# A two-layer graph kernel: row sums taken from counts, two accumulators for adj, broadcasts by transfers, and smaller edits

## The chip, the cores and the metric

The kernel runs on one core of one Trainium2 chip. The metric is the device time of one execution in microseconds. A core has five instruction streams that matter here: TensorE (PE, matrix products and transpositions), VectorE (DVE), ScalarE (ACT), GpSimd (POOL), and SyncE (SP), whose stream issues nearly all DMA transfers of this kernel. Each stream runs its instructions in program order, and waits on semaphores where an operand comes from another stream.

## What is computed

The input is `x` (3327 nodes, 256 features) and `adj` (3327 x 3327, about 0.5% of it non-zero, and the diagonal). There are two layers, each with a layer norm and a relu in front and a residual sum behind. Cut to what matters:

```python
# layer 0: h = relu(layernorm(x)); R = rows of (adj + I) scaled to sum 1
Xf = Xa = h
for n in range(2):
    logits = (Xa @ W1.T @ W2.T) @ (Xa @ W3.T).T      # 3327 x 3327
    probs = softmax(logits)
    A = probs, of each row only the largest that sum to 0.9, scaled to sum 1
    Xf = R @ Xf
    Xa = A @ Xa
    Z = Z + Xf @ U1[n].T + Xa @ U2[n].T
x = x + layernorm(h + Z)
# layer 1: h = relu(layernorm(x)), 4 heads of 64 features
hp = h @ W
e = leaky_relu(s[:, :, None] + d[:, None, :], 0.2)   # s, d: per node and head
attn = softmax(where(adj > 0, e, -inf))
x = x + elu(attn @ hp)
```

## The kernel before

The nodes are padded to 3328 and cut into 26 row tiles of 128. `adj` comes transposed, so that a tile of it can be the stationary operand of a product.

The order of the work is made by a planner at build time. Each piece of work is given to `put` with an engine, a length, a rank, the pieces that it needs, and the buffers that it takes and gives back. A list scheduler walks through modelled time, and on each engine starts the piece of smallest rank whose needs are met and whose buffers are free. The pieces are then written out in that order, so the order of each engine is fixed in the program; on the chip only the waits decide. A change of one length or need may therefore move many pieces.

**Layer 0** has two steps. At the start, `prepare` makes each row tile: layer norm, relu, projection to keys and queries (128 columns, of which one half of the partitions is keys). Half of the partitions carries one group of key tiles and the other half the others, so that two products with a contraction of 64 run side by side on the two halves of the array. `keys_summed` and `moments` (lines 722 to 753) sum the keys and their products over all row tiles: a transposition (line 730), an ACT copy (line 734), a product with 65 columns (line 739), and DVE additions (line 751). From these `stats` makes, for each row, a normal model of its logits.

For each row tile and each step, `search` (line 1343) then finds the threshold on the exponentials above which a row holds 0.9 of its sum:

- `logits` (line 842): three pairs of 512 keys, each pair on both halves of the array, and the last 255 keys on one half alone; `exps` (line 853) makes the exponentials with ACT.
- `guess` sets a first threshold from the model. An evaluation is a `count` (line 890): two ACT passes over 3327 columns with the accumulated output kept, one with Relu (how much lies below the threshold, and by how much) and one with Sign (how many lie below). `step` (lines 894 to 932) then moves the threshold: a chain of small POOL operations on one column each. Step 0 has two evaluations, step 1 three. The third of step 1 is `sum_below` on DVE (line 936), with its `step` on DVE.
- In the window around the threshold DVE selects and sorts the candidates (lines 947 and 952) and drops what lies below the cut (line 1002).

`attention` transposes the row tile's exponentials (line 1015), copies them out with ACT into `et` (line 1020), and multiplies them with the features (line 1027). Between rows, PE has `Full`: 26 matmuls per row tile of the product with adj (line 1053) into the accumulator `accf`; four adj tiles come by each transfer into `at` (line 1047); ACT copies the accumulator to `f` (line 1060), and DVE adds. The planner gives `accf` back when the copy is done. `finish2` (lines 1282 to 1302) ends a row tile of step 1: layer norm, relu, projection with the weights of layer 1, and `stage`, which makes exponentials of the score of each node and head (`qd`, `low`).

**Layer 1** is `attend_neighbours` (line 1427). It has four blocks of 832 destination columns, and in each block 26 source tiles j. For each j, SP loads the adj tiles (line 1500), ACT makes a mask of them (lines 1510 and 1511), DVE makes the exponents of four heads (line 1522), and PE multiplies them (line 1538) and sums them (line 1552). The exponents need the scores of the destination columns on all partitions: for each row tile of the block, `broadcast` transposes a score column repeated 128 times (PE, line 1460) and takes its exponential into the buffer `both` (ACT, line 1464). The large buffers of layer 1 are those of layer 0: `both` is `c`, and it is opened when all adj products are done.

The layer-1 weights are loaded by `layer1_weights` (lines 700 to 720): four transfers on SP and four products on DVE (line 713), which take two of the three `et` buffers; the planner puts them near 120 us.

## Time and profile before

| | us |
|---|---|
| median of three runs | 2310.74 (2310.22 to 2312.15) |
| the profiled execution | 2309.92 |
| its span | 2307.9 |
| PE idle in the span | 84.9 |
| PE idle, 0 to 58 | 15.5 |
| PE idle, 950 to 1100 | 3.3 |
| PE idle, 1100 to 1400 | 11.1 |
| PE idle, 1400 to 1780 | 14.2 |
| PE idle, 2000 to 2308 | 17.7 |

The profile is of one execution. The span is the time between its first and its last instruction; about 2 us of the execution lie outside it. The idle time in a stretch is its length less the busy time of PE in the table of windows. The times of PE's matmuls overlap, so a group's mean is longer than the pace at which its matmuls follow each other, and a busy PE need not be at its peak. In the groups, "x208" is the number of instructions, then come the busy time in us and the mean in ns, and then the idle time of the engine just before these instructions with what ended most of it. In a list of waits, the three numbers are the sum in us, how many waits, and the longest.

### The profile page before, as it was taken

To read this page: it belongs to the slowest core of one execution; us is meant where nothing else is said; L and a number is where in the kernel's file an instruction comes from. 1 tells how busy PE (TensorE), PEld (TensorE's weight loads), DVE (VectorE), ACT (ScalarE), POOL (GpSimd) and SP (SyncE) were. 2 spreads that over 40 slices of the span, in tenths; PEclk is the share of its full clock that TensorE was granted. 3 is DMA by queue.
4 is the path that set the end of the run, shared out by engine and by line. 5 is a ranking of instruction groups with operands and counts; after the bars stand their busy time and mean duration, and the time that the engine had idled before them with its cause. 6 is when DMAs were issued, how large, how long until landed. Compare 5 with 4: busy or idle time off the path is not lost. (4 is left out here: it accounts for less than half of the span.)

```text
span 2307.9 us, 36154 instructions
## 1 busy us (share of the span) xinstructions
PE 2223.0 (96%) x11956; PEld 1551.9 (67%) x11956; DVE 1699.8 (74%) x4299; ACT 1559.9 (68%) x2901; POOL 1017.6 (44%) x2263
## 2 busy tenths in 40 slices
PE   7989999999999999999999999999998999999997
PEld 5467777777877778777777778777877434333332
DVE  5564666656645664389889889889888797989895
ACT  5767788678777862488676787777773556565553
POOL 6345455445554541357766765677774000000000
PEclk9999999999999999999999999999999999999998
DMA  3021212212212222522212222122223343434341
GB/s 97 1 68 52 68 54 60 64 53 61 73 47 72 68 87 73 176 85 65 65 51 68 68 76 67 53 62 68 71 67 99 90 114 109 116 99 127 100 130 42
DMA packets 189654, 176.97 MB, mean 77 GB/s; under 512 B 14866, under 2 KB 145808, under 8 KB 189328
## 3 DMA queue, kind: packets, MB, share of 16 engines
q1 hardware_dynamic: 187472, 173.30, 25.8%
q8 instruction: 96, 1.57, 0.3%
q10 hardware_dynamic: 1984, 1.26, 0.2%
q14 instruction: 102, 0.84, 0.1%
HBM read 157.66 MB, written 15.89 MB: 75 GB/s over the span
## 5 line engine op out<-in xcount | busy, mean ns | idle before, releaser
L890 ACT ACTIVATE junk<-e,sc 128x3327 fp8e5<-128x3327 f32 x208 | 638.9, 3072 | 25.4 <-POOL sc L931 23.4
L1027 PE MATMUL acca<-rhs,et 128*128 128x256 f32 x2704 | 623.6, 381 | 2.3 <-ACT et L1020 2.2
L1027 PEld LDWEIGHTS acca<-rhs,et 128*128 128x128 f32 x2704 | 500.6, 191 | 66.9 <-ACT et L1020 4.8
L1053 PE MATMUL accf<-c,at 128*128 128x256 f32 x1352 | 322.8, 388 | 20.4 <-ACT f L1060 20.3
L947 DVE SCALAR_TENSOR_TENSOR y<-e,sc 128x1664 f32<-128x1664 f32 x104 | 204.6, 1967 | 187.0 <-POOL sc L928 169.3
L1053 PE MATMUL accf<-main,at 128*128 128x257 f32 x1352 | 317.0, 383 | 4.8 <-DMA at<-in_adjt_dram 4.5
L1020 ACT COPY et<-px 128x512 f32<-128x512 f32 (+1 forms) x364 | 194.4, 554 | 186.4 <-PE acca L1027 125.3
L1053 PEld LDWEIGHTS accf<-c,at 128*128 128x128 f32 x1352 | 251.6, 192 | 78.4 <-ACT f L1060 28.8
L1522 DVE SCALAR_TENSOR_TENSOR e<-c,low,et 128x832 f32<-128x832 f32 x288 | 289.1, 1075 | 16.8 <-ACT e L1592 9.5
L1053 PEld LDWEIGHTS accf<-main,at 128*128 128x128 f32 x1352 | 250.9, 191 | 46.4 <-issue 8.0
L952 DVE MAX8 cands<-y 128x8 f32<-128x208 f32 x832 | 241.1, 361 | 3.6
L1002 DVE SCALAR_TENSOR_TENSOR e<-e,thr 128x832 f32<-128x832 f32 x208 | 214.0, 1083 | 2.6 <-ACT kq L1178 0.5
L1538 PE MATMUL pl<-e,main 128*64 128x416 f32 x1152 | 212.6, 516 | 0.1
L1015 PE MATMUL px<-ident,e 128*128 128x128 f32 x1352 | 196.4, 277 | 16.8 <-ACT et L1020 7.9
L853 ACT ACTIVATE e<-pl 128x1024 f32<-128x1024 f32 x208 | 179.3, 865 | 45.6 <-PE pl L842 44.7
L1015 PEld LDWEIGHTS px<-ident,e 128*128 128x128 f32 x1352 | 163.4, 143 | 57.5 <-issue 13.6
L1511 ACT ACTIVATE et<-at 128x512 bf16<-128x512 f32 (+1 forms) x208 | 114.5, 550 | 118.3 <-DVE e L1522 76.9
L842 PE MATMUL pl<-kt,qq 64*128 64x512 f32 (+1 forms) x728 | 184.1, 588 | 0.0
L905 POOL TENSOR_SCALAR sc<-sc 128x1 f32<-128x1 f32 x104 | 40.2, 386 | 309.3 <-ACT junk L890 249.3
L1538 PEld LDWEIGHTS pl<-e,main 128*64 128x64 f32 x1152 | 79.6, 137 | 123.1 <-issue 104.0
L936 DVE SCALAR_TENSOR_TENSOR y<-e,sc 128x3327 bf16<-128x3327 f32 x26 | 95.5, 3672 | 47.9 <-POOL sc L931 47.9
L1522 DVE SCALAR_TENSOR_TENSOR rhs<-c,low,et 128x832 f32<-128x832 f32 x128 | 129.2, 1073 | 0.0
(485 smaller groups left out, 3076.8 us busy)
## 6 DMA issues: line engine op xcount, KB each, us to landing
at<-in_adjt_dram SPq DMA_DIRECT2D x416, 256.0 KB, 2.8
at<-in_adjt_dram SPq DMA_DIRECT2D x104, 192.0 KB, 3.0
at<-in_adjt_dram SPq DMA_DIRECT2D x52, 128.0 KB, 2.1
ys<-ystage SPq DMA_DIRECT2D x26, 256.0 KB, 2.4
rhs<-in_x_dram SPq DMA_DIRECT2D x26, 128.0 KB, 3.3
ystage<-in_x_dram SPq DMA_DIRECT2D x26, 128.0 KB, 2.1
base<-ys SPq DMA_DIRECT2D x26, 128.0 KB, 2.2
x1s<-ystage SPq DMA_DIRECT2D x26, 128.0 KB, 1.7
```

The lines of the kernel that those rows point to most:

```text
L842: T.matmul(pl[:, r, :m], qq[half, self.i, :], kt[half, 512 * k : 512 * k + m], start=True, stop=True,)
L853: S.activation(self.e[:, 1024 * k : 1024 * k + pl.shape[1]], pl, AF.Exp, accum_out=(self.p0, self.p1, self.p2, self.p3)[k],)
L890: S.activation(junk[:, :N], self.e[:, :N], fn, bias=t, scale=-1.0, accum_out=dst, saturate=False)
L947: V.scalar_tensor_tensor(self.y[:, : hi - lo], self.e[:, lo:hi], self.up, self.e[:, lo:hi], ALU.is_lt, ALU.mult, accum_out=(self.h0, self. ...
L952: V.max(self.cands[:, o // PIECE, :], self.y[:, o - lo : min(o + PIECE, hi) - lo])
L1002: V.scalar_tensor_tensor(piece, piece, self.thr[:, o : o + 1], piece, ALU.is_gt, ALU.mult)
L1015: T.transpose(pt[:, k, :], self.e[:, j * P : (j + 1) * P], ident)
L1020: S.copy(self.et[g][:, :m, :], self.pt.pop(g)[:, :m, :])
L1027: T.matmul(self.acc, et[:, j - 4 * g, :], rhs[self.n][:, j, :], start=(j == 0), stop=(j == NT - 1))
L1053: T.matmul(self.acc[:, : self.w], self.at[j // JC][:, j % JC, :], self.src[:, j, : self.w], start=(j == 0), stop=(j == NT - 1),)
L1522: V.scalar_tensor_tensor(held["e"][:, k, :], extra["both"][b % 2][:, k, :], low[:, j, k : k + 1], held["mask"], ALU.max, ALU.mult,)
L1538: T.matmul(q["acc"][a][k * FH : (k + 1) * FH, c, :C], main[:, j, h * FH : (h + 1) * FH], held["e"][:, h, c * C : (c + 1) * C], start=(j == 0),
```

## The change

1. **Sums from counts.** Only the first evaluation of a row has a Relu pass. Later ones have the Sign count alone, and the sum below the new threshold follows from the old one, the counts at both thresholds, and the mean of the thresholds. The third evaluation of step 1 is a Sign count on ACT in the place of `sum_below` on DVE. A few small operations of `step` move or are added, and `failures`, which decides whether a slow general path runs afterwards, looks at more of them.
2. **Two adj accumulators** in step 1: one PSUM tile with two halves of 256 columns, used in turn.
3. **Broadcasts by transfers.** `stage` makes one more exponential, `high`; each row tile stores it to a DRAM tensor `highs` (512 values of 4 bytes), and for each block two transfers bring it to all 128 partitions in `both`. The transpositions of line 1460 and the exponentials of line 1464 are gone.
4. **Buffers of layer 1.** The first block's `both` is the buffer `qq`, and the loads and masks of its first two source tiles use `kt` and `junk`; they open when all logits and counts of step 1 are done. `c` gives the second `both` and one more buffer for the exponents, which are seven now.
5. **Last keys on both halves.** The last row tile's keys lie on the second half of the array: 128 columns on the first, 127 on the second, and one column is filled by a matmul of constants whose exponential is 0. The POOL memset of that column goes.
6. **Moments** are taken from row tiles 0, 2, 4, ... alone, and scaled by their number.
7. **Layer-1 weights** are loaded by SP pieces of a later rank, apart from the products on DVE, and need the attention of step 0's fourth row tile (`done[3]`) in the plan.

The diff, cut:

```diff
+    def side(t):
+        return 1 if t == NT - 1 else t // 4 % 2
...
-        kt = wpool.tile([P, 4 * 512 - 256], F32, name="kt")
+        kt = wpool.tile([P, 3 * 512 + P], F32, name="kt")
         qq = wpool.tile([P, NT, P], F32, name="qq")
+        none = wpool.tile([P, P + 2], F32, name="none")
+        GP.memset(none, 0.0)
...
             for k in range(2):
                 for a in range(2):
...
                     )
                     lo = H * FH + a * H
...
             def copy():
-                kk = held["kk"] = kks[t % 2]
...
-                GP.memset(self.e[:, N:], 0.0)
...
-                w = min(1024, N - 1024 * k)
+                w = 512 if k < 3 else P
                 for r in range(2):
-                    m = min(512, w - 512 * r)
-                    if m > 0:
-                        half = slice(r * DA, r * DA + DA)
...
-                self.pl[k] = pl.rearrange("p r w -> p (r w)")[:, :w]
+                    m = min(w, N - 1024 * k - w * r)
+                    half = slice(r * DA, r * DA + DA)
+                    T.matmul(
+                        pl[:, r, :m],
+                        qq[half, self.i, :],
+                        kt[half, 512 * k : 512 * k + m],
+                        start=True,
+                        stop=True,
+                    )
+                    if m < w:
+                        T.matmul(pl[:, r, m:w], none[half, :P], none[half, P : P + w - m], start=True, stop=True)
+                self.pl[k] = pl[:, :, :w]
...
                 pl = self.pl.pop(k)
+                w = pl.shape[2]
                 S.activation(
-                    self.e[:, 1024 * k : 1024 * k + pl.shape[1]],
+                    self.e[:, 1024 * k : 1024 * k + 2 * w].rearrange("p (r w) -> p r w", r=2),
...
-                dst = (self.r0, self.s0)[fn == AF.Sign]
+                dst = (self.s0, self.s1, self.s2)[k] if fn == AF.Sign else self.r0
...
+                s = (self.s0, self.s1, self.s2)
+                if k == 0:
+                    TS(self.q, s[0], float(N), t, ALU.add, ALU.mult)
                     TS(B, self.r0, -2.0, self.q, ALU.mult, ALU.add)
                 else:
-                    TS(B, B, 2.0, None, ALU.mult)
+                    TS(self.q, t, (self.t0, self.t1)[k - 1], 0.5, ALU.add, ALU.mult)
+                    TS(self.u, s[k], s[k - 1], self.q, ALU.subtract, ALU.mult)
+                    TT(B, (self.B0, self.B1)[k - 1], self.u, ALU.add)
                 TS(self.d, B, -0.5, self.b, ALU.mult, ALU.add)
+                if k == self.n:
+                    TS(self.least, s[k], N - 2.0 * (WIN[self.n] - 2), BIG, ALU.is_ge, ALU.mult)
+                    TS(self.least, self.d, 0.0, self.least, ALU.is_ge, ALU.mult)
...
-            def sum_below(self):
-                y = scr.tile([P, NP], BF16, name="y")
-                V.scalar_tensor_tensor(
-                    y[:, :N], self.e[:, :N], self.t2, self.e[:, :N], ALU.is_lt, ALU.mult, accum_out=self.B2
-                )
...
             def some(self, js):
                 for j in js:
-                    if j == 0:
+                    if j == 0 and self.n == 0:
                         self.acc = ps_a.tile([P, D + 1], F32, name="accf")
+                    elif j == 0:
+                        if self.t == 0:
+                            late["accf"] = ps_a.tile([P, 2, D], F32, name="accf")
+                        self.acc = late["accf"][:, self.t % 2, :]
...
             k = plan.put("POOL", 0.35, r, keys, needs=[a])
             q = plan.put("SP", 0.2, r, double, needs=[a])
-            g = keys_summed(
+            g = t % 2 == 0 and keys_summed(
...
+                S.activation(high[:, t, :], f[:, H * FH : H * FH + H], AF.Exp, scale=1.0 - ALPHA)
+            def spread():
+                nc.sync.dma_start(highs[:, t * P : (t + 1) * P].rearrange("h p -> p h"), high[:, t, :])
...
-            return plan.put("DVE", 0.6, r, scale, needs=[a], give=["f"]), s_
+            a = plan.put("ACT", 0.92, r, stage, needs=[a], take=["f"], give=["px", "xt"])
+            h_ = plan.put("SP", 0.1, r, spread, needs=[a], lag=4.0)
+            return plan.put("DVE", 0.6, r, scale, needs=[a], give=["f"]), s_, h_
...
-                got = [plan.put("ACT", 3.05, rank - (2.1, 1.7)[j], row.count, j, fn, needs=[a]) for fn in (AF.Relu, AF.Sign)]
+                got = [
+                    plan.put("ACT", 3.05, rank - (2.1, 1.7)[j], row.count, j, fn, needs=[a])
+                    for fn in (AF.Relu, AF.Sign)[j:]
+                ]
                 a = plan.put("POOL", (3.8, 4.7)[j], rank - (2.0, 1.6)[j], row.step, j, GP, needs=[got, more])
             if EVALS[n] == 3:
-                a = plan.put("DVE", 3.65, rank - 1.3, row.sum_below, needs=[a], take=["y"], give=["y"], lag=0.02, hold=3.6)
+                a = row.pieces["counted"] = plan.put("ACT", 3.05, rank - 1.4, row.count, 2, AF.Sign, needs=[a])
                 a = plan.put("DVE", 2.7, rank - 1.3, row.step, 2, V, needs=[a])
             halves = []
...
-                    take=["accf"] * (j == 0), give=["at"] * last,
+                    take=[f.bank] * (j == 0) + ["accf"] * (n == 1 and t + j == 0), give=["at"] * last,
                 )
-            a = plan.put("ACT", 0.3, -90.0, f.copy, needs=[a], take=["f"], give=["accf"])
+            a = plan.put(
+                "ACT", 0.3, -90.0, f.copy, needs=[a], take=["f"],
+                give=[f.bank] + ["accf"] * (n == 1 and t == NT - 1),
+            )
...
             def open_heads():
-                extra["both"] = halves_of("c", None)
+                both = wpool.tile([P, NT, P], F32, name="qq").rearrange("p t d -> p (t d)")
+                extra["both"] = [both.rearrange("p (h w) -> p h w", h=H)]
+                extra["at"] = wpool.tile([P, 2 * W], F32, name="kt").rearrange("p (k w) -> p k w", k=2)
+                extra["m"] = scr.tile([P, NP // 2], BF16, name="junk").rearrange("p (k w) -> p k w", k=2)
+            def open_heads2():
+                both, e = halves_of("c", None)
+                extra["both"].append(both)
+                extra["e"] = [e]
             def open_more():
-                extra["e"] = halves_of("rhs", None)
-            opened = plan.put("SP", 0.02, 59.0, open_heads, needs=[fulls], lag=0.0)
-            more = plan.put("SP", 0.02, 59.0, open_more, needs=[freed], lag=0.0)
+                extra["e"] += halves_of("rhs", None)
+            counted = [r.pieces["counted"] for r in rows]
+            opened = [plan.put("SP", 0.02, 59.0, open_heads, needs=[logits_done, counted], lag=0.0)]
+            opened.append(plan.put("SP", 0.02, 59.0, open_heads2, needs=[fulls, opened], lag=0.0))
+            more = plan.put("SP", 0.02, 59.0, open_more, needs=[freed, opened], lag=0.0)
             def broadcast(b, rank):
                 lo, hi = b * W, (b + 1) * W
-                got = []
-                for t in range(lo // P, -(-hi // P)):
-                    held = {}
-                    def turn(t=t, held=held):
-                        held["pb"] = ps_x.tile([P, H, P], F32, name="px")
-                        for k in range(H):
-                            T.transpose(held["pb"][:, k, :], sd[:, 0, t, k : k + 1].to_broadcast([P, P]), ident)
-                    def exps(t=t, held=held):
-                        x0, x1 = max(lo, t * P), min(hi, t * P + P)
-                        S.activation(
-                            extra["both"][b % 2][:, :, x0 - lo : x1 - lo],
-                            held["pb"][:, :, x0 - t * P : x1 - t * P],
-                            AF.Exp,
-                            scale=1.0 - ALPHA,
+                got, after = [], [[ends[t][2] for t in range(lo // P, -(-hi // P))], opened[b % 2], used_heads[b % 2]]
+                for a in range(2):
+                    def fetch(a=a):
+                        nc.sync.dma_start(
+                            extra["both"][b % 2][:, 2 * a : 2 * a + 2, :],
+                            highs[2 * a : 2 * a + 2, lo:hi].partition_broadcast(P),
                         )
-                    a = plan.put("PE", 0.55, rank, turn, needs=[ends[t][0], opened, used_heads[b % 2]], take=["px"])
-                    got.append(plan.put("ACT", 0.65, rank, exps, needs=[a], give=["px"]))
...
                     held = {}
+                    def load_first(j=j):
+                        for t0, t1, w in ((0, W // P, P), (W // P, W // P + 1, W % P)):
+                            nc.sync.dma_start(
+                                extra["at"][:, j, t0 * P : (t1 - 1) * P + w].rearrange("p (i q) -> p i q", q=w),
+                                adjt[t0:t1, :, j, :w].rearrange("i p q -> p i q"),
+                            )
+                    def mask_first(j=j, held=held):
+                        held["mask"] = extra["m"][:, j, :]
+                        S.activation(extra["at"][:, j, :], extra["at"][:, j, :], AF.Relu)
+                        S.activation(held["mask"], extra["at"][:, j, :], AF.Sign)
...
-                            k = j % 6
+                            k = j % 7
...
+                        m_ = plan.put("ACT", 1.8, rank, mask_first, needs=[loads])
+                    else:
+                        loads = [
+                            plan.put("SP", 0.1, rank, load, g, needs=[logits_done], take=["at"], lag=4.0)
+                            for g in range(2)
+                        ]
+                        m_ = plan.put("ACT", 2.2, rank, mask, needs=[loads], take=own, give=["at", "at"])
...
             scaled = plan.put(
                 "DVE", 0.2, base - 50.0,
-                lambda: V.tensor_scalar(gk[:, : DA + 1], gk[:, : DA + 1], 1.0 / N, None, ALU.mult), needs=[sums],
+                lambda: V.tensor_scalar(gk[:, : DA + 1], gk[:, : DA + 1], 1.0 / (NT // 2 * P), None, ALU.mult), needs=[sums],
             )
...
                 def layer1():
-                    late["g"], late["b"], late["wa"] = layer1_weights()
-                layer1_ready = plan.put("DVE", 3.0, base + NT - 1.0, layer1, needs=[used], lag=3.0)
+                    late["g"], late["b"], late["wa"], late["a"] = layer1_loads()
+                a = plan.put("SP", 0.5, base + 4.0, layer1, needs=[used, done[3]], take=["et"], lag=8.0)
+                layer1_ready = plan.put(
+                    "DVE", 3.7, base + 5.0, lambda: layer1_scores(late["wa"], late["a"]), needs=[a], take=["et"],
+                    give=["et", "et"],
+                )
```

## The prediction

> **What bounds the kernel now.** I read the engine totals first, then the table of windows, then what TensorE waits for, then the groups of TensorE.
>
> ```profile
> span 2307.9 us, 36154 instructions
> PE 2223.0 (96%) x11956; PEld 1551.9 (67%) x11956; DVE 1699.8 (74%) x4299; ACT 1559.9 (68%) x2901; POOL 1017.6 (44%) x2263
> ```
>
> TensorE (PE) has 84.9 us of idle time in 2307.9. No other engine passes 74%, so only two things shorten the run: work taken off TensorE, and idle time taken off it. Windows (from:to; length; busy of PE, PEld, DVE, ACT, POOL; clock; DMA share; GB/s):
>
> ```profile
> 0.00:58.00 58.00, 42.55 (x248) 32.70 (x249) 31.14 (x128) 34.15 (x113) 35.95 (x123) 0.97 0.33 96
> 115.00:173.00 58.00, 49.51 (x241) 38.66 (x240) 35.81 (x122) 38.81 (x70) 24.83 (x62) 0.94 0.22 68
> ...
> 500.00:800.00 300.00, 299.67 (x1469) 234.58 (x1468) 178.47 (x527) 233.88 (x388) 155.00 (x380) 1.00 0.20 60
> ...
> 1100.00:1400.00 300.00, 288.86 (x1401) 230.79 (x1400) 264.28 (x754) 222.39 (x370) 210.44 (x420) 0.99 0.22 65
> 1400.00:1780.00 380.00, 365.84 (x1803) 297.73 (x1802) 336.21 (x960) 269.71 (x464) 259.10 (x512) 0.99 0.25 71
> 1780.00:1850.00 70.00, 66.87 (x418) 35.31 (x421) 52.66 (x75) 36.66 (x76) 6.43 (x10) 0.96 0.31 88
> 1850.00:2000.00 150.00, 150.00 (x1101) 57.77 (x1095) 138.13 (x160) 80.50 (x194) 0.00 (x0) 1.00 0.38 107
> ```
>
> Step 0 (500 to 800) leaves PE idle 0.3 us in 300. Step 1 (1100 to 1780) leaves 25 us, and there DVE is at 88%. Layer 1 (1850 to 2000) is full. The idle time stands at the start, in step 1, and at the change of layers. What PE waited for, between 950 and 1800 us:
>
> ```profile
> PE accf L1053 <- ACT f L1060: 20.3, 17, 5.1
> PE px L1015 <- ACT c L1464: 4.2, 1, 4.2
> ```
>
> In step 1 PE starts the next adj row tile only after ACT has copied the single accumulator out, and the copy queues behind a count of 3 us. The groups that the change touches:
>
> ```profile
> L890 ACT ACTIVATE junk<-e,sc 128x3327 fp8e5<-128x3327 f32 x208 | 638.9, 3072 | 25.4 <-POOL sc L931 23.4
> L936 DVE SCALAR_TENSOR_TENSOR y<-e,sc 128x3327 bf16<-128x3327 f32 x26 | 95.5, 3672 | 47.9 <-POOL sc L931 47.9
> L842 PE MATMUL pl<-kt,qq 64*128 64x512 f32 (+1 forms) x728 | 184.1, 588 | 0.0
> L1460 PE MATMUL px<-ident,sd 128*128 128x128 f32 x112 | 16.6, 281 | 0.7 <-ACT c L1464 0.5
> L739 PE MATMUL accf<-kk 128*128 128x65 f32 (+1 forms) x52 | 10.2, 279 | 0.0
> L739 PE MATMUL px<-kk 128*128 128x65 f32 (+1 forms) x52 | 9.9, 271 | 0.0
> ```
>
> Means of overlapping matmuls count time twice; I use paces from the timeline.
>
> **The Trainium skill.** "PSUM — Partial Sum Buffer", "PSUM bank collisions raise a hardware error": two engines may not touch one bank in the same partitions at once, and guarding goes by bank, not by address. The new accumulators are halves of one tile, 2 x 256 x 4 B = 2 KB of a partition, which the section "Terms" gives as one bank; so I expect PE to wait for the copy of the other half. The trace of before has one accumulator and can't show it. "TensorEngine Tiling (Array Packing)", "Instruction Overhead": a matmul of one column costs as much as one of about 60; no one-column matmul runs here yet. "DMA: Bandwidth & Descriptors", "Specifications": below 512 B a transfer does a read-modify-write, so 4-byte pieces are dear; before has none.
>
> **The change part by part.**
>
> *Counts.* In step 0 ACT loses 26 x 3.07 = 80 us; in step 1 one Relu count goes and a Sign count comes. DVE loses 95.5 us in step 1. In step 0 PE never waits for ACT, so this is worth 0 there. In step 1 it shortens no PE work; it shortens the chain of a row by one count of 3.07, and swaps 3.67 on DVE for 3.07 on ACT. PE is covered by the adj matmuls put between rows. I take 0 by itself (bounds -3 to +5).
>
> *Broadcasts by transfers.* 28 row tiles of 4 transpositions leave PE. Timeline: eight took 1.02 us, four 0.58, so 0.51 to 0.58 a tile; 28 x 0.54 = 15 us, all in stretches where PE is full. ACT loses 15.2 and gains 26 small exponentials (about 0.19 each, 5 us). Added on SP: 26 stores of 512 pieces of 4 B, and 8 loads of 852 KB (6.8 MB on 177). DMA is at 0.36 to 0.38 in layer 1, and the loads are due half a block ahead (some 55 us), so they hide. Layer 1 stays bound by PE: PE takes 4.29 us per column tile by the timeline; DVE 4 exponents at about 1.01, 4.05. Over 104 tiles that is 446 against DVE's 421 + 28 of tail work = 449, that is near balance for the block ends, so I keep 15 and give 0 to 3 back there.
>
> *Stores.* The mean packet of queue 1 took 0.258 x 16 x 2307.9 / 187472 = 51 ns; 32 pieces on each of 16 engines are 1.6 us. If a 4-byte piece costs the double, 3.3. Behind a store stand the adj loads of SP, four buffers of 4 matmuls (1.73 us) ahead: 6.9 us less the landing of 2.8 gives 4 us of cover. Cost 0 to 3 over all; I take 1.
>
> *Last keys on both halves.* Before: 255 columns on one half. After: two matmuls of 128 and 127 side by side, and one of a single column. Timeline: 8 matmuls of logits in 1.99 us, 6 in 1.55; with 0.48 per pair the old last one costs about 0.5, the new group, with one fixed price more, about 0.4. 52 x 0.1 = 5 us (bounds -3 to +10). POOL loses 52 memsets.
>
> *Moments.* 26 of 52 tiles lose a transposition and two 65-column products on PE, about 0.11 + 0.2: 0.3 us. 13 in step 0's stream: 4 us; 13 in the start, which has idle time: 3.
>
> *Two accumulators.* If the halves were independent all 20.3 us would go. As built, the ACT copy of one half stands among the matmuls of the next. In 14 of 25 successions it comes early, or 12 attention matmuls (5 us) stand before the next use; in 11, PE goes on for 2 to 6 matmuls (0.9 to 2.6 us) and then waits. Without a start ahead the wait ranges over the rest of a count plus the copy, 0.4 to 3.5; with 1.75 us ahead its mean is 1.75 x 1.75 / 2 / 3.1 = 0.5, so 11 x 0.5 = 5.4, say 7 with what else stays. Gain 13 (bounds 0 to 20).
>
> *Buffers of layer 1.* The first exponents now stand before the last row's finish and no longer wait for all of step 1. The 4.2 us and three waits of 0.7 to 0.9 at 1774 to 1807 go: 7 us (bounds 3 to 8). Seven buffers for e instead of six: 0, since PE is not short of e in the middle.
>
> *Layer-1 weights moved.* They took two `et` buffers at 120 us while DVE waited 5.7 us for gat_w, and PE lost 5.3:
>
> ```profile
> 130.50 1.11 PE L1015 MATMUL px<-ident,e 128*128 128x128 f32 x4 [5.32 <-ACT et L1020]
> ```
>
> This goes; with the first row a count shorter I take 7 (bounds 4 to 10). The loads come later on SP and hold one of three `et` for about 6 us: up to 2 lost, I take 2 with the stores' 1 making 3.
>
> Sum against the profiled run: 2307.9 - 15 - 4 - 3 - 5 - 13 - 7 - 7 + 3 = 2257. The profiled execution took 2309.92, 2.0 outside the span; the median shown, 2310.74, is 2.8 above the span. 2257 + 2.8 = 2260. Own range: logits from +3 to -10, stalls 0 to 20, tail 0 to 3 back: mostly 2250 to 2272.
>
> **The rivals.**
>
> *One bank, one wait (0.20).* In favour: 11 waits are built in, and ACT now holds a third Sign count in step 1, so a copy may find three long counts instead of a DVE pass. Then 11 waits cost 1.5 to 2 each, the 20 us stay, and layer 1 gives 3 back at block ends: about 2278. Against: ACT's sum in step 1 is unchanged.
>
> *More gain (0.10).* Stalls vanish, the last keys save 0.2 each, and the start gets 10: about 2245. Against: the waits in the built order.
>
> *Small pieces clog the queue (0.07), the slower side.* A store of `high` blocks SP's queue and the DMA engines between adj loads. PE lost 4.5 us once in step 0 for an adj load, so the cover can fail. It takes back the 51 us at 2 us of PE idle per row tile; that needs a store of about 4 + 2 = 6 us beyond its neighbours, 190 ns or more for a 4-byte piece against the mean of 51. With 280 ns a store takes 9 us, 3 more than the break-even, 26 x 3 = 78 in all less 51: 2330 or so. The double for read-modify-write doesn't get there.
>
> *The change doesn't do what it says (0.03).* If estimates from trapezoids led rows out of their window, the slow general path would run, or rows take the same time with the gains eaten by a new order: about 2310. The step's own equations take the same sums of the data, so I give it little.
>
> **How the numbers follow.** The forecast has 0.60. 0.2% (4.6 us) is about what a measurement of this kernel can tell from no change. Faster: 0.60 + 0.20 + 0.10 = 0.90; same 0.03; slower 0.07. The range for 8 in 10 holds the forecast's own, most of the first rival and half of the second: 2238 to 2288.
>
> **What would show it.** PE's busy time falls to about 2195 and its share stays at 96 to 98%. The group of transpositions from `sd` is gone. The wait of accf for f falls to 7 in about 11; at 18 or more the first rival holds. PE's wait for `et` near 130 us and that for c at 1780 are gone. The logits group is at about 180 by the timeline, with twice the small forms. The stores of `high` land in under 4 us; above 7, with PE waiting for `at`, the slower rival holds. A time above 2288 means a new wait in step 1 or on DVE in layer 1; one below 2238 means that I priced the start or the logits too low.

## The result

| | median us (range) | ratio to before, 95% interval |
|---|---|---|
| before, timed beside it | 2310.60 (2310.22 to 2312.15) | |
| changed | 2366.99 (2364.74 to 2369.41) | 1.0243 (1.0225 to 1.0261) |

The change costs 56 us, where 51 us less were forecast. From the page of the changed kernel:

```profile
span 2362.9 us, 36052 instructions
PE 2222.6 (94%) x11974; PEld 1562.7 (66%) x11974; DVE 1618.3 (68%) x4229; ACT 1459.7 (62%) x2817; POOL 939.1 (40%) x2214
q1 hardware_dynamic: 203376, 180.10, 31.1%
L1075 PE MATMUL accf<-c,at 128*128 128x256 f32 x1352 | 342.8, 403 | 79.2 <-DMA at<-in_adjt_dram 75.5
base<-ys SPq DMA_DIRECT2D x26, 128.0 KB, 8.3
```

The last three lines before:

```profile
q1 hardware_dynamic: 187472, 173.30, 25.8%
L1053 PE MATMUL accf<-c,at 128*128 128x256 f32 x1352 | 322.8, 388 | 20.4 <-ACT f L1060 20.3
base<-ys SPq DMA_DIRECT2D x26, 128.0 KB, 2.2
```

DVE and ACT lost 81 and 100 us of work, roughly as forecast (the prediction took 95.5 from DVE, and from ACT 80 and about 10). PE's busy time did not fall, and its idle time rose from 84.9 to 140.3 us, the whole difference of the spans. The new idle time stands before the adj products of step 1 (79.2 us, against 20.4 before), and it is the adj tile in `at` that comes late. PE's waits in step 1:

```profile
PE accf L1075 <- DMA at<-in_adjt_dram: 75.5, 22, 6.1
PE acca L1043 <- ACT et L1036: 3.7, 12, 0.3
PE accf L1075 <- ACT f L1082: 3.6, 7, 0.8
```

The wait for the accumulator's copy (20.3 us before) is nearly gone, as forecast; a wait for a transfer took its place. `base`, a load that before landed in 2.2 us, takes 8.3. The issues of DMAs show why. First the store's line in the page's list of DMA issues (times, KB each, median us to landing); then, from the timeline of one row tile, what SP issued (start, length), and PE's first matmuls that needed it:

```profile
highs<-high SPq DMA_DIRECT2D x26, 2.0 KB, 9.6
```

```profile
1503.99 0.33 SPq L1064 DMA_DIRECT2D at<-in_adjt_dram  x1
1505.72 0.38 SPq L1323 DMA_DIRECT2D highs<-high  x1
1508.20 2.05 SPq L1064 DMA_DIRECT2D at<-in_adjt_dram  x2
1510.31 0.43 SPq L1086 DMA_DIRECT2D base<-ys  x1
```

```profile
1518.00 2.07 PE L1075 MATMUL accf<-c,at 128*128 128x256 f32 x4 [3.34 <-DMA at<-in_adjt_dram]
```

A store of 2 KB takes 9.6 us. The adj tiles issued at 1508.20, 2.5 us behind it, reach PE only at 1518, 9.8 us after their issue; the median adj load of 256 KB lands in 2.9. PE then waits 3.34 us, and its next four matmuls take 2.07 us where four of the same took 1.03 at 1512.8. The Trainium skill ("TensorE: Matmul & The Clock Gate", "What's actually happening") says that an idle window of about 3.4 us sends TensorE back to half its clock; the trace agrees: the granted clock is 0.50 from 1517.5 to 1520.9, around the end of this wait of 3.34 us, and 0.95 on average from 1100 to 1400 (0.99 before). In step 1 it falls to a half 16 times, against 4 before. This fits the 20 us by which the group `accf<-c` is longer than before (342.8 against 322.8). It fits, too, that PE's busy time did not fall: without the late transfers it does, to 2178.5 us in the run e13 below.

Where the 55 us of span came from: the changed kernel gains 20 us up to the end of step 0, loses 72 in step 1 and the change of layers, and 3 in layer 1. The three stretches are cut at the last group of adj matmuls of step 0 and at the first product of layer 1; the runs below are in the same table, since the experiments are read from it.

| us | start and step 0 | step 1 and change of layers | layer 1 | span |
|---|---|---|---|---|
| before | 968.2 | 839.2 | 500.5 | 2307.9 |
| changed | 948.5 | 911.1 | 503.3 | 2362.9 |
| e1_turned | 942.9 | 815.9 | 496.8 | 2255.6 |
| e3_pe_bcast | 946.3 | 814.2 | 499.3 | 2259.8 |
| e8_old_counts | 953.0 | 838.9 | 506.3 | 2298.2 |
| e9_dve_third | 945.5 | 821.2 | 505.4 | 2272.1 |
| e13_block_turn | 947.0 | 795.5 | 494.8 | 2237.3 |
| e14_no_tail | 947.2 | 816.1 | 487.5 | 2250.8 |
| e15_before_two_acc | 966.0 | 827.6 | 508.0 | 2301.6 |

### The profile page after: what moved, and what is told of

Same layout as the page of the kernel before. It is cut to its first block, busy times and chain, and to the rows that moved or that the text cites. A ratio compares the mean times of both kernels' runs of the same rounds, so it can differ in the third digit from the quotient of the medians.

```text
span 2362.9 us, 36052 instructions
## 1 busy us (share of the span) xinstructions
PE 2222.6 (94%) x11974; PEld 1562.7 (66%) x11974; DVE 1618.3 (68%) x4229; ACT 1459.7 (62%) x2817; POOL 939.1 (40%) x2214
## 5 line engine op out<-in xcount | busy, mean ns | idle before, releaser
L908 ACT ACTIVATE junk<-e,sc 128x3327 fp8e5<-128x3327 f32 x182 | 559.1, 3072 | 40.2 <-POOL sc L953 38.6
L1075 PE MATMUL accf<-c,at 128*128 128x256 f32 x1352 | 342.8, 403 | 79.2 <-DMA at<-in_adjt_dram 75.5
L1075 PEld LDWEIGHTS accf<-c,at 128*128 128x128 f32 x1352 | 261.8, 201 | 129.5 <-DMA at<-in_adjt_dram 78.3
L1561 ACT ACTIVATE et<-at 128x448 bf16<-128x448 f32 (+1 forms) x204 | 112.3, 550 | 130.7 <-DVE e L1572 76.5
L1588 PE MATMUL pl<-e,main 128*64 128x416 f32 x1024 | 189.3, 519 | 2.2 <-DVE e L1572 2.1
L857 PE MATMUL pl<-kt,qq 64*128 64x512 f32 (+1 forms) x832 | 175.0, 539 | 0.0
L1082 ACT COPY f<-accf 128x257 f32<-128x257 f32 (+1 forms) x52 | 19.3, 372 | 231.0 <-PE accf L1075 231.0
L684 POOL TENSOR_SCALAR mv<-mv 128x1 f32<-128x1 f32 x78 | 47.1, 604 | 227.5 <-DVE mv L679 135.4
L1572 DVE SCALAR_TENSOR_TENSOR e<-c,low,et 128x832 f32<-128x832 f32 x128 | 128.6, 1074 | 5.4 <-PE accf L1602 3.2
L1560 ACT ACTIVATE at<-at 128x448 f32<-128x448 f32 (+1 forms) x204 | 109.9, 539 | 32.1 <-DMA at<-in_adjt_dram 31.9
```

The costliest lines, as they stand in the source:

```text
L857: T.matmul(pl[:, r, :m], qq[half, self.i, :], kt[half, 512 * k : 512 * k + m], start=True, stop=True,)
L908: S.activation(junk[:, :N], self.e[:, :N], fn, bias=t, scale=-1.0, accum_out=dst, saturate=False)
L1075: T.matmul(self.acc[:, : self.w], self.at[j // JC][:, j % JC, :], self.src[:, j, : self.w], start=(j == 0), stop=(j == NT - 1),)
L1572: V.scalar_tensor_tensor(held["e"][:, k, :], extra["both"][b % 2][:, k, :], low[:, j, k : k + 1], held["mask"], ALU.max, ALU.mult,)
L1588: T.matmul(q["acc"][a][k * FH : (k + 1) * FH, c, :C], main[:, j, h * FH : (h + 1) * FH], held["e"][:, h, c * C : (c + 1) * C], start=(j == 0),
```

## The experiments

Theory: the forecast's other terms hold, and the store of `high` alone, by holding up the adj loads, turns a gain of 50 us into a loss. Rivals: the new order delays the loads; or another part of the change (bank, buffers) loses too. The diffs below are cut to the lines that matter. "e1", "e2" and so on are the runs; each ratio is to the kernel before.

### The store, taken away and added

**e1_turned**: scores made in turned form, so that they are stored as runs of 512 bytes.

```diff
+                for k in range(2):
+                    T.matmul(
+                        pm[:H, F + 2 * H :], late["wa"][:, k, F : F + H], held["xt"][:, k, :], start=(k == 0), stop=(k == 1)
+                    )
-                S.activation(high[:, t, :], f[:, H * FH : H * FH + H], AF.Exp, scale=1.0 - ALPHA)
+                S.activation(hi, held["pm"][:H, H * FH + 2 * H :], AF.Exp, scale=1.0 - ALPHA)
-                nc.sync.dma_start(highs[:, t * P : (t + 1) * P].rearrange("h p -> p h"), high[:, t, :])
+                nc.sync.dma_start(highs[:, t * P : (t + 1) * P], held["hi"])
```

> The changed kernel, but the scores that go to DRAM are made already turned: two more products of 128 columns in finish2 give 4 x 128 scores, one exponential of 4 partitions follows, and a row tile is stored as 4 pieces of 512 bytes instead of 512 pieces of 4. Theory (the small pieces hold up the adj loads behind them): the store lands in about 2 us, PE's 80.8 us of waits for at fall under 10, and so does the slow restart after them; the time falls from 2367 to 2255 to 2275. Rival (the new order of loads and the added traffic of 6.8 MB delay the adj loads, not the form of the store): the waits stay above 50 us and the time above 2330.

Measured: 2260.80 us (2257.43 to 2262.99), ratio 0.9787 (0.9771 to 0.9803). PE's waits for `at` over the whole run, in the changed kernel and in e1:

```profile
PE accf L1075 <- DMA at<-in_adjt_dram: 80.8, 23, 6.1
```

```profile
PE accf L1074 <- DMA at<-in_adjt_dram: 4.6, 1, 4.6
```

The planner's pieces and lengths are those of the changed kernel, so the order is the same: the form of the store, with the two products that it needs, is worth 106 us, and the first rival falls.

**e2_before_store**: the kernel before, with the exponential and the store only (and their entries in the plan).

```diff
+                S.activation(high[:, t, :], f[:, H * FH : H * FH + H], AF.Exp, scale=1.0 - ALPHA)
+                nc.sync.dma_start(highs[:, t * P : (t + 1) * P].rearrange("h p -> p h"), high[:, t, :])
```

> The kernel before, with one thing added: the exponential high and its store of 512 pieces of 4 bytes per row tile, which nothing reads. Theory: the store alone makes PE wait for at about 3 us per row tile, as in the changed kernel; 2310 becomes 2380 to 2410. Rival (the stores hurt only in the changed order): under 2330.

Measured: 2360.94 us (2360.11 to 2362.72), ratio 1.0220 (1.0203 to 1.0237); the store lands in 10.6 us. So 26 small stores that nothing reads cost 50.6 us, less than the range expected. PE's waits for `at` rise from 4.5 to 37.2 us in all, while those for `f` fall from 20.6 to 14.2: a part of the delay falls into waits that were there.

```profile
PE accf L1055 <- DMA at<-in_adjt_dram: 37.2, 10, 5.9
```

**e4_act_queue**: the changed kernel with the same store issued by ACT, in the plan too.

```diff
-                nc.sync.dma_start(highs[:, t * P : (t + 1) * P].rearrange("h p -> p h"), high[:, t, :])
+                nc.scalar.dma_start(highs[:, t * P : (t + 1) * P].rearrange("h p -> p h"), high[:, t, :])
```

> The changed kernel with the store of high issued from ACT instead of SP. If the loads wait for the store in SP's own queue, moving it frees them: waits for at under 15 us, about 2265 to 2280. If the pieces stop the DMA engines or the memory for all queues, the waits stay at 60 us or more and the time at 2345 to 2375.

Measured: 2392.51 us (2391.76 to 2393.52), ratio 1.0354 (1.0336 to 1.0371), above the range expected; the store lands in 10.7 us, and PE's waits are longer:

```profile
PE accf L1075 <- DMA at<-in_adjt_dram: 104.7, 20, 7.2
```

The store does not hold the loads up by standing ahead of them in SP's queue: from another queue it does the same and more.

**e5_before_16b** and **e6_before_spaced** change nothing of e2 but where the pieces lie in DRAM:

```diff
-    highs = spill.tile([H, NP], F32, name="highs")
+    highs = spill.tile([NP, H], F32, name="highs")
-                nc.sync.dma_start(highs[:, t * P : (t + 1) * P].rearrange("h p -> p h"), high[:, t, :])
+                nc.sync.dma_start(highs[t * P : (t + 1) * P, :], high[:, t, :])
```

```diff
-    highs = spill.tile([H, NP], F32, name="highs")
+    highs = spill.tile([NP, H, P], F32, name="highs")
-                nc.sync.dma_start(highs[:, t * P : (t + 1) * P].rearrange("h p -> p h"), high[:, t, :])
+                nc.sync.dma_start(highs[t * P : (t + 1) * P, :, 0], high[:, t, :])
```

> As the run of the kernel before with the store added, but the DRAM tensor is laid out by node, so that a row tile's 2 KB go as 128 pieces of 16 bytes instead of 512 of 4. If the cost goes by the number of pieces, a quarter of the 50.6 us remains or less: 2312 to 2325. If any store under 512 bytes a piece stops the engines for a fixed time, the time stays above 2340.

> As the run of the kernel before with the store added, 512 pieces of 4 bytes as there, but each piece lies 512 bytes from the next in DRAM instead of side by side. If the pieces are slow because neighbours fall into the same piece of memory, the stall shrinks: under 2325. If each small piece has its own price wherever it lies, the time stays at 2350 to 2375.

Measured: 2305.95 us (2304.02 to 2307.39), ratio 0.9986 (0.9980 to 0.9993), and 2305.77 us (2303.67 to 2309.05), ratio 0.9985 (0.9979 to 0.9992). Both cost nothing; e5 is even below its range. (They are even 3 us faster than before. The added pieces also move the planner's order, which is the likely reason; it was not tested apart.) Their landing times, from the lists of DMA issues of e2, then e5, then e6:

```profile
highs<-high SPq DMA_DIRECT2D x26, 2.0 KB, 10.6
```

```profile
highs<-high SPq DMA_DIRECT2D x26, 2.0 KB, 2.3
```

```profile
highs<-high SPq DMA_DIRECT2D x26, 2.0 KB, 2.2
```

e2 and e6 have the same plan and write the same 512 pieces of 4 bytes; in e6 they lie 512 bytes apart, and 55 us are gone. So neither the number of pieces nor their size is enough by itself. Nor is it enough that pieces touch: those of 16 bytes in e5 lie side by side too. What does it is very small pieces side by side, 128 of them in 512 bytes in e2 against 32 in e5. The records of single packets say the same, and who pays:

```
                     packets of 4 B (mean ns)   packets of 2048 B: mean ns, over 1 us
before               14035 (9.0)                112.0,   1
changed              27891 (8.5)                148.6, 598
e2_before_store      27763 (8.5)                150.0, 564
e5_before_16b        14451 (9.0)                114.5,  29
e6_before_spaced     27763 (8.5)                114.9,   3
```

The pieces themselves are quick: in e4, where the stores have ACT's queue almost to themselves, a packet of 4 bytes takes 8.0 ns in the mean. It is the packets of 2048 bytes, most of them of adj tiles, that stand still, up to 8.9 us each in the changed kernel. In e5 a trace of this is left: 29 packets over 1 us, none over 1.9. What in the memory makes neighbours collide, whether the size of the pieces or their number in one place counts, and from which distance on they do no harm, was not tried.

### The broadcasts

**e3_pe_bcast**: the changed kernel with `high`, its stores and its loads taken out, and PE's transpositions and ACT's exponentials back.

```diff
+                    a = plan.put("PE", 0.55, rank, turn, needs=[ends[t][0], opened[b % 2], used_heads[b % 2]], take=["px"])
+                    got.append(plan.put("ACT", 0.65, rank, exps, needs=[a], give=["px"]))
-                    got.append(plan.put("SP", 0.1, rank, fetch, needs=[after], lag=7.0 + 5.0 * a))
```

> The changed kernel with the broadcasts on PE and ACT again (no high, no stores, no loads of it), everything else kept. Theory: all the other parts keep what the prediction gave them, less the 15 us of the broadcasts: about 2275 (2262 to 2290). Rival (other parts lose too, such as the two halves in one bank or the moved buffers): 2300 or more.

Measured: 2263.40 us (2261.58 to 2264.36), ratio 0.9797 (0.9780 to 0.9813). With the stores gone and everything else kept, no other part loses, so the second rival falls too. But e3 is only 2.6 us slower than e1, where the broadcasts were to be worth 15. One part of the answer is e1's own price: its two extra products pace at 0.53 us per row tile, 26 x 0.53 = 13.8 us of PE in step 1. **e13_block_turn** takes that away: six or seven row tiles are turned by one transposition, and PE spends 1.1 us on the four of them.

```diff
+                    T.transpose(held["ph"][: n * H], sd[:, 0, t0:t1, :].rearrange("p t h -> p (t h)"), ident)
+                    S.activation(held["hi"][: n * H], held["ph"][: n * H], AF.Exp, scale=1.0 - ALPHA)
+                    for t in range(t0, t1):
+                        k = (t - t0) * H
+                        nc.sync.dma_start(highs[:, t * P : (t + 1) * P], held["hi"][k : k + H, :])
```

> The changed kernel, with the scores of six or seven row tiles turned by one transposition on PE and one exponential, four times in all, then stored as pieces of 512 bytes. Against the version with turned scores this takes 26 x 0.53 = 13.8 us of products off PE in step 1 and puts 4 x 0.1 there. Theory (step 1 is now bound by PE): 2245 to 2251. Rival (step 1 is bound by the rows' chain all the same): 2256 to 2262.

Measured: 2238.53 us (2237.05 to 2240.89), ratio 0.9689 (0.9674 to 0.9704), below the range expected. It is the fastest version of this study, 72 us under the kernel before. Against e1 it gains 22.3 us, more than the 13.8 of the products; where the rest comes from is open. Against e3, which has the broadcasts on PE, it gains 24.9 us. Of the 22.5 between the two spans, 18.7 lie in step 1 and the change of layers, where e3 has 13.8 us from the last adj group to the first product and e13 0.3, and 4.5 in layer 1.

**e14_no_tail** asks why layer 1 gains so little. It leaves out, in blocks 0 to 2, DVE's reciprocals and additions (with them the residual sum and the scaling of three quarters of the output).

```diff
                     def invert(m=m, held=held, b=b):
+                        if b < 3:
+                            return
                     def add(m=m, held=held, b=b):
+                        if b < 3:
+                            return
```

> The version with turned scores (2260.8), leaving out, for blocks 0 to 2 of layer 1, DVE's reciprocals, the last two additions of each row tile and so the residual sum (the elu's exponentials stay, with a constant scale). Theory (DVE, with its tail work and its waits at the block ends, sets the period of a block at 118.85 us, where PE's own work is about 114): the period falls to 113 to 115 and the time to 2246 to 2252. Rival (the release of the exponents' buffers in groups of three sets it, whatever DVE does besides): 2257 or more.

Measured: 2252.77 us (2251.20 to 2254.00), ratio 0.9751 (0.9736 to 0.9766). The time is a little above the range expected, but layer 1 falls by 9.3 us, from 496.8 to 487.5, and the time from one block to the next from 118.85 to 115.5 us (121.2 before). The chain of waits at a block's end, first of e1, then of e14 (start, length, what):

```profile
2004.82 0.48 PE px L1674 x3
2005.30 0.83 PE acca L1607 x8
2006.13 0.74 PE accf L1607 x8
2006.90 0.48 DVE e L1577
2007.90 1.08 DVE e L1577
2009.08 1.97 DVE e L1577 x2
2011.75 0.43 DVE ystage L1690
2012.20 0.42 DVE ystage L1691
2012.72 1.87 DVE c L1577 x2
...
2021.30 1.09 DVE rhs L1577
2022.43 1.61 PE pl L1593 x6
```

```profile
2009.81 0.70 PE acca L1607 x8
2010.50 0.70 PE accf L1607 x8
2011.20 0.48 PE px L1674 x3
2011.68 1.55 PE pl L1593 x8
2013.23 0.48 PE px L1674 x3
2013.70 4.34 PE pl L1593 x24
```

In e1 the chain of waits crosses to DVE from 2006.9 to 2022.4: its exponents wait for PE's sums to free a buffer, and its tail work stands between them. In e14 it stays on PE.

**e10_pool_adds** moved those additions to POOL instead.

```diff
+                            GP.tensor_scalar(y[:m, 1], y[:m, 1], 1.0, -1.0, ALU.min, ALU.add)
+                            GP.tensor_add(y[:m, 0], y[:m, 0], y[:m, 1])
+                            GP.tensor_add(y[:m, 0], y[:m, 0], held["x1"][:m])
```

> The version with turned scores (2260.8), with the last additions of layer 1's blocks 0 to 2 on POOL (three operations of 128 x 256) instead of two on DVE. If DVE at the ends of the blocks is what ate the broadcasts' 15 us (21 tiles x 0.85 us = 18 us less on DVE): 2250 to 2256. If DVE isn't what PE is late for, or POOL slows DVE: 2258 to 2270.

Measured: 2260.22 us (2257.71 to 2261.99), ratio 0.9783 (0.9766 to 0.9799): no gain. POOL's operations are long (206 us in layer 1), and beside them two of DVE's exponents take 2.54 us instead of 2.05. So DVE's busy time over layer 1 falls by only 4 us (438.2 to 433.8), and the run tells nothing against e14.

### The counts and the accumulators

**e8_old_counts**: e1 with the counts of before. **e9_dve_third**: e1 with only the third evaluation on DVE as before. They differ from each other by the Relu pass of the second evaluation.

```diff
-                    for fn in (AF.Relu, AF.Sign)[j:]
+                    for fn in (AF.Relu, AF.Sign)
-                a = row.pieces["counted"] = plan.put("ACT", 3.05, rank - 1.4, row.count, 2, AF.Sign, needs=[a])
+                a = row.pieces["counted"] = plan.put("DVE", 3.65, rank - 1.3, row.sum_below, needs=[a], take=["y"], give=["y"], lag=0.02, hold=3.6)
```

> The version with turned scores (2260.8), with the counts of the kernel before: Relu and Sign in both evaluations, and the third of step 1 by sum_below on DVE. Prediction's value for the counts: 0 (bounds -3 to +5), so 2258 to 2266. Rival (ACT's and DVE's shorter work is what lets the copies and exponentials come in time in step 1): 2270 or more, with PE's waits for ACT and DVE in step 1 back above 15 us.

> The version with turned scores (2260.8), with the third evaluation of step 1 by sum_below on DVE again (26 x 3.67 = 95 us back on DVE, 80 off ACT), the second evaluation still without its Relu pass. If DVE's load in step 1 is what the new counts relieve, most of the 39 us that the old counts cost comes back: 2285 to 2302. If the Relu pass on ACT, in each row's chain, is what counts: 2258 to 2270.

Measured: e8 2300.07 us (2299.76 to 2302.39), ratio 0.9963 (0.9949 to 0.9977); e9 2275.06 us (2270.53 to 2276.36), ratio 0.9841 (0.9825 to 0.9858). The counts are worth 39 us: 14 by the third evaluation, which lies between the two expectations for it, and 25 by the Relu pass, which e8 has back in both steps. Where the time stands in e8, by PE's waits in step 1 and the windows:

```profile
PE px L1033 <- DVE e L1020: 20.6, 3, 12.7
PE accf L1077 <- ACT f L1084: 6.7, 14, 0.6
```

```profile
1500.00:1716.00 216.00, 214.62 (x1101) 173.58 (x1098) 189.64 (x535) 164.33 (x289) 147.91 (x289) 1.00 0.24 67
1716.00:1792.00 76.00, 46.68 (x213) 36.29 (x213) 64.50 (x180) 35.89 (x57) 38.84 (x72) 0.82 0.25 82
```

Until 1716 PE is full, since it takes adj products ahead. Then these are used up, and PE waits 29 us in 76 for the last rows. The rows' own chain (counts, steps, window) sets the pace; PE's filler hides it only for so long. This is shown for the 23 us that e8 loses against e1 in step 1 and the change of layers. Of the spans' other difference, 10 us stand in the start and step 0, where the forecast saw none, and 9.5 in layer 1; the order of the plan also moves these cuts (in e8 products of step 1's last rows stand behind the first product of layer 1), and the causes were not looked for.

**e7_one_accumulator** undoes the two halves in e1; **e16_block_turn_one** in e13; **e15_before_two_acc** adds them to the kernel before.

```diff
-                    if j == 0:
+                    if j == 0 and self.n == 0:
                         self.acc = ps_a.tile([P, D + 1], F32, name="accf")
+                    elif j == 0:
+                        if self.t == 0:
+                            late["accf"] = ps_a.tile([P, 2, D], F32, name="accf")
+                        self.acc = late["accf"][:, self.t % 2, :]
```

> The version with turned scores (2260.8), with one adj accumulator in step 1 as in the kernel before. Theory (the two halves save what the prediction gave them, about 13 us of waits for the copy): 2270 to 2280, with 15 to 20 us of PE's waits for f back. Rival (both halves lie in one bank, so they save nothing; the other edits shortened step 1): 2257 to 2264.

> As the block-wise turned version, with one adj accumulator as in the kernel before. If the two halves save nothing once the counts are shorter, as with the tile-wise turned version (2257.6 against 2260.8): within 3 us of the block-wise version. If they help where PE alone bounds step 1: 5 us slower or more.

> The kernel before with the two accumulators in step 1 alone. The prediction's step: PE's waits for f fall from 20.3 us to about 7 and the time by 13: 2297. What the last runs suggest (the rows' chain on ACT and DVE sets the pace of step 1, and PE's waits for f are only where its spare time shows): waits for f fall, as much idle time comes back elsewhere in step 1, and the time stays within 4 us of 2310.6.

Measured: e7 2257.59 us (2255.23 to 2258.47), ratio 0.9772 (0.9756 to 0.9788), 3.2 us faster than e1; e16 2242.88 us (2242.03 to 2244.33), ratio 0.9710 (0.9695 to 0.9724), 4.3 us slower than e13. In both pairs the intervals overlap, and opposite signs of this size may be the planner's order alone. e15 2302.95 us (2301.48 to 2303.43), ratio 0.9968 (0.9955 to 0.9980), 7.5 us faster than before. PE's waits in step 1 in e15, and its last window there:

```profile
PE px L1015 <- ACT et L1020: 10.5, 11, 2.7
PE accf L1059 <- ACT f L1066: 8.2, 17, 0.9
```

```profile
1720.00:1794.00 74.00, 55.73 (x261) 41.75 (x262) 62.07 (x165) 38.58 (x68) 33.93 (x59) 0.88 0.09 26
```

The waits for `f` fall by 12 us, from 20.3 to 8.2, as forecast. But with them gone PE runs through its adj products earlier, and 18 us of idle time stand in the last 74 before layer 1. The time lies between the two expectations.

### The small parts

**e11_old_weights** puts the layer-1 weights back to their early place; **e12_old_keys** takes the moments from all row tiles and the last keys on one half.

```diff
+                    layer1_scores(late["wa"], late["a"])
+                layer1_ready = plan.put("DVE", 3.0, base + NT - 1.0, layer1, needs=[used], lag=3.0)
```

```diff
-            g = t % 2 == 0 and keys_summed(
+            g = keys_summed(
-                w = 512 if k < 3 else P
+                w = min(1024, N - 1024 * k)
```

> The version with turned scores (2260.8), with the layer-1 weights loaded and multiplied in one piece at the early place, as in the kernel before. The prediction gave the move 7 us with the first row's shorter chain, of which 5.3 is PE's wait for et: 2265 to 2269. Rival (the wait was hidden): within 2 us of 2260.8.

> The version with turned scores (2260.8), with the sums of keys over all row tiles and the last 255 keys on one half of the array, as in the kernel before. The prediction gave these 4 + 3 + 5 = 12 us: 2268 to 2277. Rival (step 1 is bound by the rows, so only step 0's share counts): 2263 to 2268.

Measured: e11 2267.27 us (2266.12 to 2267.49), ratio 0.9809 (0.9793 to 0.9826), so 6.5 us; PE's wait for `et` is back (7.8 us in all, the longest 4.9). e12 2272.57 us (2271.29 to 2273.52), ratio 0.9832 (0.9815 to 0.9848), so 11.8 us. Both as forecast.

## Why the prediction was wrong

**Stores, the step that failed.** The prediction took "32 pieces on each of 16 engines" at 51 ns, 1.6 us, doubled that to 3.3, and found 4 us of cover; "Cost 0 to 3 over all; I take 1." A store takes 9.6 us, and undoing its form is worth 106 us (e1), 128 with a cheaper turn (e13). The rival on the slower side had the place right: the store, and PE waiting for `at`, 80.8 us or 3.1 per row tile. Its chance of 0.07 came from the price. Its sum was off: 6 us as the break-even already holds the 51 us of gain, so 3 us beyond it, 78 in all, are to be added to 2310, which gives about 2388 and not "2330 or so"; 2367 was measured. The price per piece was the wrong quantity for forecast and rival alike: a piece took 8 ns, less than the 51 of the mean packet, and the cost fell on the packets behind. The prediction also left out that PE restarts at half clock (20 us) and that layer 1's first masks come late (ACT waits 8.5 us for their adj tiles behind the store at 1857.9; layer 1 at 503.3 against e1's 496.8). The sentence it leaned on, from the Trainium skill's "DMA: Bandwidth & Descriptors", "Specifications" (read-modify-write below 512 bytes), does not tell these cases apart: pieces of 16 bytes, and of 4 bytes apart, are below 512 too and cost nothing here. The measurement decides.

**Counts.** Forecast 0 with bounds of -3 and +5; measured 39. "PE is covered by the adj matmuls put between rows" was true row by row and false over the step: the cover is a stock that runs out. The high share of DVE (88%) in step 1 was a sign that the chain had little to spare, and was read past; but only 14 of the 39 us go with the pass on DVE, and 25 with the Relu pass on ACT.

**Accumulators.** Forecast 13; measured 7.5 in the kernel before, 4.3 and -3.2 in the changed ones; these two are not clear of noise. The wait fell as worked out (20.3 to 8.2); a part came back at the end of the step. The one bank did not keep PE's waits at 18 or more: 8.2 us in e15, where no waits for `at` cover them, so the rival of the bank falls.

**Broadcasts and buffers.** Forecast 15 and 7. e13 against e3, both with the moved buffers, gives 24.9 for the broadcasts, but not where the forecast put it ("all in stretches where PE is full"): 18.7 lie in step 1 and the change of layers. In layer 1 itself 4.5 us were gained instead of 11 (21 of the 28 row tiles at 0.54). DVE's work at the block ends, priced at "0 to 3", is the likely reason: without it e14 gains 9.3 there. The moved buffers were undone in no run, so their 7 stand unmeasured.

**Last keys, moments, weights.** 12 and 7 forecast, 11.8 and 6.5 measured.

Without the store's form the changed kernel takes 2260.8, and the forecast was 2260. That is partly chance: the counts' 39 missing make up for the accumulators, for e1's extra products and for layer 1. Undoing parts one at a time gives more than the 72 us they give together; that they share the same idle time fits this, and is not shown.

## What to carry to other kernels

When a transfer scatters small pieces, ask whether they fall side by side in DRAM, and look at the landing time of the loads behind it, not only at its own; turning the data on chip first, in one go for many tiles, cost almost nothing here. Filler work hides a slow chain only while there is filler: compare the pace of the chain with that of the engine over the whole stage, and doubt any edit to the chain that is priced at nothing. A wait that ends is only gained if the stage's slowest chain gets shorter with it.

## What was not expected of the hardware

512 pieces of 4 bytes written side by side land in 9.6 to 10.6 us, and 564 to 598 of a run's 43392 packets of 2048 bytes, most of them adj loads, then take over 1 us; the same pieces 512 bytes apart land in 2.2 us, and 3 packets do. Pieces of 16 bytes side by side land in 2.3 us, and 29 do, at no cost. From ACT's queue the effect is larger (104.7 us of PE's waits against 80.8 from SP's).
